# An LSTM grid and a landmark attention in one kernel: LSTM weights, states and row buffers ahead of the group statistics, SP in written order, four edge products at once

## The chip, the cores and the metric

One core of a Trainium2 chip. The metric is the device time of one execution in microseconds (us), lower is better; the time of a kernel is the median of its runs. Profiles show one profiled execution.

## The reference

The input x is 16 images of 64 x 64 pixels with 128 features, in fp32. The reference does three things in a row; each adds its result to its input:

```python
x = x + lstm(group_norm(x))           # two-dimensional LSTM: each pixel needs the pixel above and the one to the left
t = tokens(x)                         # 16 x 4096 x 128
t = t + attention(layer_norm(t))      # 8 heads of 16, 64 landmarks
t = t + ffn(layer_norm(t))            # Wx, batch norm, then y[t] = sigmoid(wx[t] + y[t-1] @ V.T)
```

`group_norm` takes mean and variance for each image over groups of four features and all pixels. The LSTM has five gates, each with weights w (input), u (state) and a bias b. The attention is the Nyström kind: `out = softmax(q kl) @ pinv(softmax(ql kl)) @ (softmax(ql k) @ v)` where ql and kl are means over 64 tokens, and then `res`, a convolution of v along the tokens with 33 taps for each head, is added before the output product.

## The kernel before

All of it runs as one program. TensorE (PE) is the busiest engine; VectorE (DVE), ScalarE (ACT), GpSimd (POOL) and the queue of SyncE (SP) work beside it. The stages follow one another:

1. **Front end.** `attention_tiles` and `conv_bands` (L592) prepare constants of the attention. `conv_bands` writes the taps of each head into a padded line in DRAM (`cb_flat`) and reads it back with overlapping rows into `cb_tm` (L611, on ACT's queue, 128 partitions x 8 heads of 768 bytes). For each head, PE turns it (`cb_t`, L619 to L622) into a band matrix (128 x 128) and two corners, and DVE copies these to `bands` and `edges` (L623, L625). A band product handles what one tile of 128 tokens takes from itself, the corners what it takes from its two neighbours.
2. **Group statistics** (`group_stats`, L32). For each of 16 images a load of 2 MB (`gs_xb`, L56, three buffers) on SP's queue, 32 transposes on PE into banks of PSUM (L61), eight `bn_stats` on DVE (L62), one aggregate (L63). At the end a few small operations, and on POOL the power that gives `grstd` (L29, a helper).
3. **LSTM** (`lstm_grid`, L81). The grid is walked by diagonals; a diagonal of more than 32 pixels is split in two units by images, 190 units in all. A unit has up to four tiles of 128 rows. `load` (L170) fetches x rows (`ls_xt`), `enter` (L175) transposes and normalises them, `gate_x` and `gate_h` (L192, L196) make the gates' products in PSUM, ACT applies sigmoid and tanh (L200), DVE and POOL update cell and state, `turn`, `measure`, `factors` and `normalise` make the output row and its layer norm, `store` (L242) writes it, and `collect` adds it to the landmark sums `acc`. In `slot(t)` (L269) pieces of seven units are interleaved by hand: it loads unit t+5, computes unit t and stores unit t-3. The block `tc.manual_schedule` (L304) keeps PE, DVE, ACT and POOL in the written order. SP is not in the list, so the scheduler places SP's transfers: in the built program the first 18 loads of `ls_xt` stand ahead of the loads of the group statistics, and the LSTM's weights (L105 to L115) and zeroed states (L117 to L123) are issued after the statistics.
4. **Landmarks**: means, inverses.
5. **Attention** (`attention`, L696). An image is eight groups of 512 tokens. `step(s)` (L1061) is written by hand and interleaves several groups: `new` is projected to K, Q and V (`project`, L801) and its largest scores are found (`greatest`, L838), `mid`, one image behind, makes its weights against the landmarks and sums V (`weigh` L865, `values` L884), `nxt` and `cur`, two images behind, compare, soften and attend (L949, L980, L992), `prev` goes on to the next layer (`turn_output`, `feed` L1046). PE, DVE, ACT and POOL keep the written order. PSUM has eight banks of 128 x 512 fp32, each a buffer of its own (`bank(k, ...)`): a product into a bank waits until the last reader of the bank's former content is done.
   In this stage, `project` puts V of a group into bank 2; ACT copies it to SBUF (`at_v`, L814) and DVE copies it in head order to `VH` (`at_vh`, L816), the source of the convolution. `greatest` then uses banks 0, 1, 2, 3. The convolution of a quarter of the heads over half an image is done in each step: `convolve` (L908) makes two band products into one bank (bank 7, or bank 3 in step 3, where it stands in `project`'s `last()` slot), `convolve_edges` (L919) adds four corner products (32 x 32, over two row groups) into the same bank, and ACT copies the bank to `R` (L931). `gather` (L933, bank 4, at the end of an image) and `output` (L1017, bank 6) use other banks.
6. **Recurrence** of the last layer.

The corner products of the kernel before:

```python
first, last = slice(0, E), slice(P - E, P)
for rows, tok, d in ((last, first, -1), (first, last, 1)):
```

Both heads of a pair use the same two row groups of 32 rows, the first and the last.

Of the kernel before, what the change touches and what calls it, by code (L numbers as in the profile page):

```python
# [77 lines left out]
        inv_std(nc, cp, grstd, var, mhalf, "gs")  # L78


def lstm_grid(nc, tc, x, w, u, bias, ident, mhalf, gmean, grstd, t1, acc):  # L81

# [12 lines left out]
    xv = x.rearrange("b i j f -> (i j) b f")  # L95
    tv = t1.rearrange("b n f -> n b f")
    with ExitStack() as ctx:
        cp = ctx.enter_context(tc.tile_pool(name="ls_c", bufs=1))
        ld = ctx.enter_context(tc.tile_pool(name="ls_ld", bufs=AHEAD + 4))
        wk = ctx.enter_context(tc.tile_pool(name="ls_wk", bufs=2))  # L100
        sm = ctx.enter_context(tc.tile_pool(name="ls_sm", bufs=4))
        ps_z = ctx.enter_context(tc.tile_pool(name="ls_psz", bufs=5, space=PSUM))
        ps_t = ctx.enter_context(tc.tile_pool(name="ls_pst", bufs=1, space=PSUM))

        wt, ut, bt = [], [], []  # L105
        for g in range(5):
            a = cp.tile([P, P], F32, name=f"ls_w{g}")
            nc.sync.dma_start(out=a, in_=w[g])
            wt.append(a)
            a = cp.tile([P, P], F32, name=f"ls_u{g}")  # L110
            nc.sync.dma_start(out=a, in_=u[g])
            ut.append(a)
            a = cp.tile([P, 1], F32, name=f"ls_b{g}")
            nc.sync.dma_start(out=a, in_=bias[g].rearrange("(p o) -> p o", o=1))
            bt.append(a)  # L115

        hs = [cp.tile([P, S, D0 + 1, HB], F32, name=f"ls_h{k}") for k in range(2)]  # L117
        cs = [cp.tile([P, S, D0 + 1, HB], F32, name=f"ls_cell{k}") for k in range(2)]
        for a in (*hs, *cs, acc):
            nc.vector.memset(a, 0.0)  # L120
        rows = [cp.tile([P, KT, 2 * F + 4], F32, name=f"ls_tt{k}") for k in range(7)]
        for a in rows:
            nc.vector.memset(a[:, :, F : F + 4], 1.0)  # L123

        class Unit:
            pass
# [175 lines left out]
                    gate_x(after, g)  # L302

        with tc.manual_schedule(  # L304
            engines={mybir.EngineType.PE, mybir.EngineType.DVE, mybir.EngineType.Activation, mybir.EngineType.Pool}
        ):
            for t in range(AHEAD):
                load(units[t])
            for t in range(2):
                enter(units[t])  # L310
            for r in ready[-1]:
                add_states(r)
            for g in (0, 1, 2, 4, 3):
                gate_x(units[0], g)
            for t in range(len(units) + 4):
                slot(t)
# [275 lines left out]
def conv_bands(nc, tc, conv_w, dram, bands, edges):  # L592

    H, _, KS, _ = conv_w.shape
    E = edges.shape[2]
    first = P - 1 + KS // 2
    width = P + 2 * E
    row = P + width  # L600
    with ExitStack() as ctx:
        sp = ctx.enter_context(tc.tile_pool(name="cb_s", bufs=1))
        ps = ctx.enter_context(tc.tile_pool(name="cb_ps", bufs=2, space=PSUM))
        flat = dram.tile([H, row], F32, name="cb_flat")
        line = sp.tile([H, row], F32, name="cb_line")
# [5 lines left out]
        nc.scalar.dma_start(out=tm, in_=bass.AP(tensor=flat.tensor, offset=flat.offset, ap=[[1, P], [row, H], [1, width]]))  # L611
        turn = sp.tile([P, P], F32, name="cb_turn")
        nc.gpsimd.memset(turn, 0.0)
        nc.gpsimd.affine_select(
            out=turn, in_=turn, compare_op=ALU.not_equal, fill=1.0, base=1 - P, pattern=[[1, P]], channel_multiplier=1
        )
        for h in range(H):
            t = ps.tile([P, 2, P], F32, tag="t", name="cb_t")
            nc.tensor.matmul(t[:, 0, :], tm[:, h, E : E + P], turn, start=True, stop=True)  # L619
            before, after = slice(P - E, P), slice(0, E)  # L620
            nc.tensor.matmul(t[before, 1, 0:E], tm[:, h, 0:E], turn[:, 0:E], start=True, stop=True)
            nc.tensor.matmul(t[after, 1, 0:E], tm[:, h, P + E :], turn[:, P - E :], start=True, stop=True)  # L622
            nc.vector.tensor_copy(bands[:, h], t[:, 0, :])  # L623
            for rows in (before, after):
                nc.vector.tensor_copy(edges[rows, h], t[rows, 1, 0:E])  # L625
# [70 lines left out]
def attention(nc, tc, t1, gamma, beta, wqkv, ident, mhalf, fixed, xp, rows, qm, km, pinvT, t2, wx, wx_stats, out):  # L696
# [20 lines left out]
    with ExitStack() as ctx:  # L717
# [10 lines left out]

        bands, edges, wo, bo, wfT, ones, ones_b, minus, ident_b, heads, vs, R, split, tops, avs = fixed

        def quarter(n):
            return slice(n * W2, (n + 1) * W2)

# [67 lines left out]
        def project(gr, last):  # L801

            k, q, v = banks(0, 1, 2)
            nc.tensor.matmul(k, wqkv[:, P : 2 * P], gr.xT, start=True, stop=True)
            gr.KT = big.tile([P, GC], F32, tag="KT", name="at_KT", bufs=Q + 1)
            nc.scalar.copy(gr.KT, k)
            nc.tensor.matmul(q, wqkv[:, 0:P], gr.xT, start=True, stop=True)
            gr.QT = big.tile([P, GC], F32, tag="QT", name="at_QT", bufs=2 * Q + 1)
            nc.scalar.mul(gr.QT, q, 0.25)
            for c in range(C):  # L810
                cs = slice(c * P, (c + 1) * P)
                nc.tensor.matmul(v[:, cs], gr.xT[:, cs], wqkv[:, 2 * P : 3 * P], start=True, stop=True)
            gr.V = big.tile([P, C, F], F32, tag="V", name="at_v", bufs=Q + 1)
            nc.scalar.copy(gr.V.rearrange("p c f -> p (c f)"), v)  # L814
            last()
            nc.vector.tensor_copy(  # L816
                gr.im.VH[:, :, gr.tiles, :].rearrange("p h k d -> p k h d"), v.rearrange("p (k h d) -> p k h d", k=C, h=H)
            )

        def extras(mid, cur):  # L820

# [62 lines left out]
        def values(gr):  # L884


            im = gr.im
            p = bank(6, [P, P])
            for c in range(C):
                for n in range(NP):  # L890
                    nc.tensor.matmul(
                        p[quarter(n)], gr.V[:, c, quarter(n)], gr.e[:, n, c, :],
                        start=(c == 0), stop=(c == C - 1), skip_group_check=True,
                    )
            if gr.g == 0:
                nc.vector.tensor_copy(im.sums, p)
            else:
# [10 lines left out]
        def convolve(im, half, pair, k):  # L908

            lo, hi = half * K // 2, (half + 1) * K // 2  # L910
            im.cv = bank(k, [P, 2, K // 2, DH])
            for j in range(2):
                h = 2 * pair + j

                nc.tensor.matmul(
                    im.cv[:, j], bands[:, h, :], im.VH[:, h, lo:hi], start=(j == 0), stop=True, skip_group_check=True
                )

        def convolve_edges(im, half, pair):  # L919

            lo, hi = half * K // 2, (half + 1) * K // 2
            for j in range(2):
                h = 2 * pair + j
                first, last = slice(0, E), slice(P - E, P)
                for rows, tok, d in ((last, first, -1), (first, last, 1)):
                    a, z = max(lo, -d), min(hi, K - d)
                    nc.tensor.matmul(
                        im.cv[tok, j, a - lo : z - lo], edges[rows, h, :], im.VH[rows, h, a + d : z + d],
                        start=False, stop=True, skip_group_check=True,
                    )  # L930
            nc.scalar.copy(R[:, lo:hi, 2 * pair : 2 * pair + 2, :].rearrange("p k h d -> p h k d"), im.cv)  # L931

        def gather(im):  # L933

            at = bank(4, [P, C, P])
            nc.tensor.transpose(at[:, 0, :], im.sums, ident)
            for n in range(NP):
                nc.tensor.matmul(at[:, 1, W2 * n : W2 * n + 2], im.total[:, n, :], ones[:, 0:2], start=True, stop=True)
# [122 lines left out]
        def step(s):  # L1061
# [309 lines left out]
def kernel(ctx: ExitStack, tc: tile.TileContext, ins: dict, out: bass.AP):  # L1371
# [25 lines left out]
    with tc.tile_pool(name="at_c", bufs=1) as ac, tc.tile_pool(name="at_x", bufs=1) as xp, tc.tile_pool(  # L1397
# [45 lines left out]
```

## Time and profile before

| | |
|---|---|
| median of 3 runs | 4115.65 us (4110.36 to 4120.33) |
| the profiled execution | 4127.1 us, its span 4125.6 us |
| mean granted clock of PE | 0.975 |
| busy in the span | PE 3937.3 (95%), DVE 2956.8 (72%), POOL 2783.7 (67%), ACT 2527.9 (61%) |
| DMA | 383.82 MB in 493553 packets, mean 93 GB/s |

The stages in the trace, by windows (us from the start): 0 to 113 front end and group statistics, 113 to 1520 LSTM, 1520 to 1718 landmarks, 1718 to 1840 the first 16 steps of the attention, 1840 to 3600 its steady part, 3600 to 3815 its end, 3815 to 4126 the recurrence.

How to read rows of the profile: a row of a timeline has the start in us, the length in us of what is grouped, the engine, the line of the program, the operation, output and input, the shapes and the count; in brackets stands how long the engine was idle before, and which instruction it waited for. SPq and ACTq are the queues on which SP and ACT issue transfers; PEld is the loading of weights into PE, which overlaps PE's products. The ends of products overlap, so the cost of a piece of PE's work is read from its start to the next piece's start.

### The profile page before, as it was taken

To read this page: it belongs to the slowest core of one execution; us is meant where nothing else is said; L and a number is where in the kernel's file an instruction comes from. 1 tells how busy PE (TensorE), PEld (TensorE's weight loads), DVE (VectorE), ACT (ScalarE), POOL (GpSimd) and SP (SyncE) were. 2 spreads that over 40 slices of the span, in tenths; PEclk is the share of its full clock that TensorE was granted. 3 is DMA by queue.
4 is the path that set the end of the run, shared out by engine and by line. 5 is a ranking of instruction groups with operands and counts; after the bars stand their busy time and mean duration, and the time that the engine had idled before them with its cause. 6 is when DMAs were issued, how large, how long until landed. Compare 5 with 4: busy or idle time off the path is not lost. (4 is left out here: it accounts for less than half of the span.)

```text
span 4125.6 us, 99034 instructions
## 1 busy us (share of the span) xinstructions
PE 3937.3 (95%) x37518; PEld 2651.4 (64%) x37518; DVE 2956.8 (72%) x7152; ACT 2527.9 (61%) x4973; POOL 2783.7 (67%) x4189
## 2 busy tenths in 40 slices
PE   7899999999999989889999999999999999988697
PEld 5767665555667678656666666666666666655486
DVE  8677777777787775437777777777777777757465
ACT  0466655555666654346666666666666666755597
POOL 0577776777777763247878778787877788787133
PEclk9799999999999989999999999999999999999798
DMA  8123222223232210112333332333333233222799
GB/s 341 43 69 81 78 76 78 78 79 83 76 82 77 72 40 4 45 32 77 83 90 86 86 92 80 92 82 90 88 84 93 80 93 82 81 73 82 234 265 174
DMA packets 493553, 383.82 MB, mean 93 GB/s; under 512 B 35208, under 2 KB 466192, under 8 KB 491024
## 3 DMA queue, kind: packets, MB, share of 16 engines
q1 hardware_dynamic: 473840, 341.82, 28.7%
q0 software_dynamic: 17728, 34.61, 4.7%
q8 instruction: 299, 4.90, 0.5%
q14 instruction: 182, 1.49, 0.1%
q10 hardware_dynamic: 1504, 0.99, 0.1%
HBM read 172.82 MB, written 204.48 MB: 91 GB/s over the span
## 5 line engine op out<-in xcount | busy, mean ns | idle before, releaser
L200 ACT ACTIVATE ls_g<-ls_z,ls_b 128x304 f32<-128x304 f32 (+26 forms) x950 | 509.1, 548 | 372.5 <-PE ls_z L198 336.0
L906 POOL TENSOR_TENSOR at_total<-at_total,at_e 128x512 f32<-128x512 f32 x480 | 611.0, 1273 | 131.7 <-ACT at_e L882 102.8
L194 PE MATMUL ls_z<-ls_xn,ls_w 128*128 128x304 f32 (+26 forms) x1900 | 611.3, 470 | 8.2 <-DMA ls_w<-in_L_conv_wf_dram 5.2
L194 PEld LDWEIGHTS ls_z<-ls_xn,ls_w 128*128 128x128 f32 x1900 | 341.8, 196 | 184.5 <-issue 84.6
L778 POOL TENSOR_SCALAR at_T<-at_T,at_nb 128x128 f32<-128x128 f32 x512 | 403.5, 796 | 13.3
L845 DVE TENSOR_REDUCE at_mxq<-at_bank 128x1 f32<-128x512 f32 x512 | 328.6, 683 | 113.0 <-PE at_bank L842 112.9
L198 PE MATMUL ls_z<-ls_hsum,ls_u 128*128 128x304 f32 (+26 forms) x1140 | 371.6, 463 | 0.0
L280 POOL TENSOR_TENSOR ls_g<-ls_g,ls_cell 128x304 f32<-128x304 f32 (+26 forms) x190 | 175.8, 926 | 280.9 <-ACT ls_g L200 256.0
L961 DVE TENSOR_REDUCE at_cmx<-at_bank 128x8 f32<-128x512 f32 x512 | 317.6, 684 | 59.0 <-PE at_bank L954 58.6
L882 ACT ACTIVATE at_e<-at_bank 128x512 f32<-128x512 f32 x512 | 264.3, 603 | 114.1 <-PE at_bank L876 114.1
L990 ACT ACTIVATE at_eT<-at_bank 128x512 f32<-128x512 f32 x512 | 264.3, 603 | 95.7 <-PE at_bank L987 95.7
L198 PEld LDWEIGHTS ls_z<-ls_hsum,ls_u 128*128 128x128 f32 x1140 | 213.8, 196 | 128.6 <-issue 78.2
L237 ACT ACTIVATE ls_tt<-ls_tt,ls_nb 128x128 f32<-128x128 f32 (+9 forms) x632 | 261.0, 479 | 4.1 <-POOL ls_nb L232 4.1
L198 PE MATMUL ls_z<-ls_h,ls_u 128*128 128x304 f32 (+26 forms) x760 | 259.9, 465 | 2.1 <-DVE ls_h L288 1.9
L228 POOL TENSOR_TENSOR ls_tt<-ls_ve,mhalf 128x4 f32<-128x4 f32 (+2 forms) x190 | 228.5, 1203 | 15.2
L281 DVE TENSOR_TENSOR ls_g<-ls_g,ls_g 128x304 f32<-128x304 f32 (+26 forms) x190 | 98.4, 518 | 194.7 <-POOL ls_g L280 193.5
L1259 DVE SCALAR_TENSOR_TENSOR rc_y<-rc_w,rc_scale,rc_z 128x256 f32<-128x256 f32 x344 | 155.3, 481 | 108.1 <-PE rc_z L1246 107.1
L1246 PE MATMUL rc_z<-rc_y,rc_vT 128*128 128x256 f32 x688 | 186.0, 408 | 40.4 <-ACT rc_y L1267 28.8
L816 DVE COPY at_vh<-at_bank 128x512 f32<-128x512 f32 x128 | 88.5, 692 | 185.9 <-ACT at_v L814 154.6
L1042 ACT ACTIVATE at_z<-at_u,at_nb,at_r 128x128 f32<-128x128 f32 x512 | 211.6, 504 | 11.5 <-POOL at_nb L1037 11.5
L229 POOL TENSOR_TENSOR ls_tt<-ls_ve,mhalf 128x4 f32<-128x4 f32 (+2 forms) x190 | 214.3, 1128 | 0.0
L1052 ACT COPY at_fx<-at_bank 128x512 f32<-128x512 f32 x128 | 132.7, 1037 | 125.5 <-DVE wx_stats L1050 100.4
(249 smaller groups left out, 9651.3 us busy)
## 6 DMA issues: line engine op xcount, KB each, us to landing
t<-ls_tt SPq DMA_DIRECT2D x392, 130.0 KB
at_T<-t SPq DMA_DIRECT2D x128, 264.0 KB
gs_xb<-in_x_dram SPq DMA_DIRECT2D x16, 2048.0 KB
at_xh<-t SPq DMA_DIRECT2D x128, 256.0 KB
t<-at_u SPq DMA_DIRECT2D x128, 256.0 KB
out_dram<-at_u SPq DMA_DIRECT2D x128, 256.0 KB
wx<-at_fx SPq DMA_DIRECT2D x128, 256.0 KB
rc_w<-wx SPq DMA_DIRECT2D x64, 512.0 KB
```

Of the source, the lines that this page charges most:

```text
L194: nc.tensor.matmul(v.z[g][:, : v.cols], wt[g], v.xn, start=True, stop=False)
L198: nc.tensor.matmul(view(v, v.z[g]), ut[g], hin, start=False, stop=True)
L200: nc.scalar.activation(a[:, : v.cols], v.z[g][:, : v.cols], AF.Tanh if g == 4 else AF.Sigmoid, bias=bt[g])
L228: nc.gpsimd.tensor_tensor(v.tt[:, 0:k, F + 2], ve[:, 0, :k], mhalf[:, :k], ALU.pow)
L229: nc.gpsimd.tensor_tensor(v.tt[:, 0:k, F + 3], ve[:, 1, :k], mhalf[:, :k], ALU.pow)
L237: nc.scalar.activation(v.tt[:q, k, F + 4 :], v.tt[:q, k, 0:F], AF.Identity, bias=v.nb[:q, k : k + 1], scale=v.tt[:q, k, F + 3 : F + 4],)
L778: nc.gpsimd.tensor_scalar(x[:, c, :], x[:, c, :], gr.nbt[:, 0, c : c + 1], gr.nbt[:, 1, c : c + 1], ALU.mult, ALU.subtract)
L845: nc.vector.tensor_reduce(gr.im.mxq[:, n : n + 1, gr.g], gr.s[n], AX.X, ALU.max)
L882: nc.scalar.activation(gr.e[:, n].rearrange("p c m -> p (c m)"), s[n], AF.Exp)
L906: nc.gpsimd.tensor_tensor(total, total, e[:, :, c, :], ALU.add)
L961: nc.vector.tensor_reduce(gr.mx[:, n].rearrange("p j c -> p c j"), gr.s[n].rearrange("p (c j m) -> p c j m", c=C, j=2), AX.X, ALU.max)
L990: nc.scalar.activation(gr.eT[:, n], s[n], AF.Exp)
```

## The change

- **LSTM.** Weights, biases, zeroed states and row buffers become a function of their own, `lstm_tiles`. It is called before `group_stats`, in a pool that is opened before it; the weights are now issued on ACT's queue. The zeroing of `acc` stays in `lstm_grid`.
- **SP in written order**: `group_stats` runs in a block that keeps SP in order, and the LSTM's block has SP in its list. The LSTM's pools get their waits by tile. In the built program, the statistics' loads `gs_xb` now stand ahead of the x rows of the LSTM; the first three do not wait for PE, and the first load of x rows waits for the last readers of the statistics' memory.
- **VH** is copied from `gr.V` in SBUF instead of from the bank, in three copies; odd heads get the two halves of the partitions exchanged, and `conv_bands` makes their bands and corners to match (two half-height products in place of one for an odd head).
- **Convolution**: the two heads of a pair go to two banks (7 and half of the bank 6 that `values` uses; 2 and 3 in step 3), and the four corner products use four different row groups. `R` is filled by two ACT copies, one for each bank. `values` leaves its sums in bank 6 until after the convolution (`keep_values`). `output` moves from bank 6 to 4, `gather` from 4 to 5.

```diff
+def lstm_tiles(nc, cp, shape, w, u, bias):
...
+        nc.scalar.dma_start(out=a, in_=w[g])
...
+    for a in (*hs, *cs):
+        nc.vector.memset(a, 0.0)
...
-def lstm_grid(nc, tc, x, w, u, bias, ident, mhalf, gmean, grstd, t1, acc):
+def lstm_grid(nc, tc, x, fixed, ident, mhalf, gmean, grstd, t1, acc):
...
-        ld = ctx.enter_context(tc.tile_pool(name="ls_ld", bufs=AHEAD + 4))
+        ld = ctx.enter_context(tc.tile_pool(name="ls_ld", bufs=AHEAD + 4, reuse_waits="tile"))
...
         with tc.manual_schedule(
-            engines={mybir.EngineType.PE, mybir.EngineType.DVE, mybir.EngineType.Activation, mybir.EngineType.Pool}
+            engines={
+                mybir.EngineType.PE, mybir.EngineType.DVE, mybir.EngineType.Activation, mybir.EngineType.Pool,
+                mybir.EngineType.SP,
+            }
         ):
+            nc.vector.memset(acc, 0.0)
...
-            before, after = slice(P - E, P), slice(0, E)
+            before, after = ((slice(mid - E, mid), slice(mid, mid + E)) if mid else (slice(P - E, P), slice(0, E)))
...
-            nc.vector.tensor_copy(
-                gr.im.VH[:, :, gr.tiles, :].rearrange("p h k d -> p k h d"), v.rearrange("p (k h d) -> p k h d", k=C, h=H)
-            )
+            to = gr.im.VH[:, :, gr.tiles, :].rearrange("p (n j) k d -> p j k n d", j=2)
+            by = gr.V.rearrange("p k (n j d) -> p j k n d", j=2, d=DH)
+            nc.vector.tensor_copy(to[:, 0], by[:, 0])
+            for rows, other in ((low, high), (high, low)):
+                nc.vector.tensor_copy(to[rows, 1], by[other, 1])
...
-            p = bank(6, [P, P])
+            gr.six = bank(6, [P, 2, 2 * P])
+            p = gr.six[:, 0, 0:P]
...
-            im.cv = bank(k, [P, 2, K // 2, DH])
+            im.cv = [a.rearrange("p (k d) -> p k d", d=DH) for a in of]
...
-                first, last = slice(0, E), slice(P - E, P)
-                for rows, tok, d in ((last, first, -1), (first, last, 1)):
+                for rows, tok, d in ((quarter(3 - 2 * j), quarter(0), -1), (quarter(2 * j), quarter(3), 1)):
...
-            nc.scalar.copy(R[:, lo:hi, 2 * pair : 2 * pair + 2, :].rearrange("p k h d -> p h k d"), im.cv)
+            for j in range(2):
+                nc.scalar.copy(R[:, lo:hi, 2 * pair + j, :], im.cv[j])
...
-            at = bank(4, [P, C, P])
+            at = bank(5, [P, C, P])
...
-            p = bank(6, [P, C, F])
+            p = bank(4, [P, C, F])
...
-                    convolve(*conv, 3)
+                    convolve(*conv, [a[:, 0 : 2 * P] for a in banks(2, 3)])
...
-                convolve(*conv, 7)
+                convolve(*conv, [bank(7, [P, 2 * P]), mid.six[:, 1] if mid else bank(6, [P, 2 * P])])
+            if mid:
+                keep_values(mid)
...
-            group_stats(nc, tc, x, ident, mhalf, gmean, grstd)
...
-            lstm_grid(nc, tc, x, *lw, ident, mhalf, gmean, grstd, t1, acc)
+            with tc.tile_pool(name="ls_c", bufs=1) as lc:
+                lstm_fixed = lstm_tiles(nc, lc, (B, D0, F), *lw)
+                with tc.manual_schedule(engines={mybir.EngineType.SP}):
+                    group_stats(nc, tc, x, ident, mhalf, gmean, grstd)
+                lstm_grid(nc, tc, x, lstm_fixed, ident, mhalf, gmean, grstd, t1, acc)
```

More of the change, by code (lines that the diff above doesn't have):

```diff
@@ L78, in group_stats @@
         inv_std(nc, cp, grstd, var, mhalf, "gs")
-def lstm_grid(nc, tc, x, w, u, bias, ident, mhalf, gmean, grstd, t1, acc):
+def lstm_tiles(nc, cp, shape, w, u, bias):
+    B, D0, F = shape
+    S = 2
+    HB = B // S
+    KT = D0 * HB // P
+    wt, ut, bt = [], [], []
+    for g in range(5):
+        a = cp.tile([P, P], F32, name=f"ls_w{g}")
+        nc.scalar.dma_start(out=a, in_=w[g])
+        wt.append(a)
+        a = cp.tile([P, P], F32, name=f"ls_u{g}")
+        nc.scalar.dma_start(out=a, in_=u[g])
+        ut.append(a)
+        a = cp.tile([P, 1], F32, name=f"ls_b{g}")
+        nc.scalar.dma_start(out=a, in_=bias[g].rearrange("(p o) -> p o", o=1))
+        bt.append(a)
+    hs = [cp.tile([P, S, D0 + 1, HB], F32, name=f"ls_h{k}") for k in range(2)]
+    cs = [cp.tile([P, S, D0 + 1, HB], F32, name=f"ls_cell{k}") for k in range(2)]
+    for a in (*hs, *cs):
+        nc.vector.memset(a, 0.0)
+    rows = [cp.tile([P, KT, 2 * F + 4], F32, name=f"ls_tt{k}") for k in range(7)]
+    for a in rows:
+        nc.vector.memset(a[:, :, F : F + 4], 1.0)
+    return wt, ut, bt, hs, cs, rows
+def lstm_grid(nc, tc, x, fixed, ident, mhalf, gmean, grstd, t1, acc):
     B, D0, D1, F = x.shape
@@ L97, in lstm_grid @@
     with ExitStack() as ctx:
-        cp = ctx.enter_context(tc.tile_pool(name="ls_c", bufs=1))
-        ld = ctx.enter_context(tc.tile_pool(name="ls_ld", bufs=AHEAD + 4))
[L100 to L123, printed above, removed]
+        ld = ctx.enter_context(tc.tile_pool(name="ls_ld", bufs=AHEAD + 4, reuse_waits="tile"))
+        wk = ctx.enter_context(tc.tile_pool(name="ls_wk", bufs=2, reuse_waits="tile"))
+        sm = ctx.enter_context(tc.tile_pool(name="ls_sm", bufs=4, reuse_waits="tile"))
+        ps_z = ctx.enter_context(tc.tile_pool(name="ls_psz", bufs=5, space=PSUM, reuse_waits="tile"))
+        ps_t = ctx.enter_context(tc.tile_pool(name="ls_pst", bufs=1, space=PSUM, reuse_waits="tile"))
+        wt, ut, bt, hs, cs, rows = fixed
         class Unit:
@@ L618, in conv_bands @@
             t = ps.tile([P, 2, P], F32, tag="t", name="cb_t")
-            nc.tensor.matmul(t[:, 0, :], tm[:, h, E : E + P], turn, start=True, stop=True)
-            before, after = slice(P - E, P), slice(0, E)
+            mid = P // 2 if h % 2 else 0
+            for i in range(0, P, mid or P):
+                n, c = mid or P, E + (i + mid) % P
+                nc.tensor.matmul(t[i : i + n, 0, :], tm[:, h, c : c + n], turn, start=True, stop=True)
+            before, after = ((slice(mid - E, mid), slice(mid, mid + E)) if mid else (slice(P - E, P), slice(0, E)))
             nc.tensor.matmul(t[before, 1, 0:E], tm[:, h, 0:E], turn[:, 0:E], start=True, stop=True)
@@ L729, in attention @@
         bands, edges, wo, bo, wfT, ones, ones_b, minus, ident_b, heads, vs, R, split, tops, avs = fixed
+        low, high = slice(0, P // 2), slice(P // 2, P)
         def quarter(n):
@@ L884, in values @@
         def values(gr):
-            im = gr.im
-            p = bank(6, [P, P])
+            gr.six = bank(6, [P, 2, 2 * P])
+            p = gr.six[:, 0, 0:P]
             for c in range(C):
@@ L894, in values, with keep_values @@
                     )
+        def keep_values(gr):
+            im, p = gr.im, gr.six[:, 0, 0:P]
             if gr.g == 0:
@@ L906, in add_weights, with convolve @@
                 nc.gpsimd.tensor_tensor(total, total, e[:, :, c, :], ALU.add)
-        def convolve(im, half, pair, k):
+        def convolve(im, half, pair, of):
             lo, hi = half * K // 2, (half + 1) * K // 2
-            im.cv = bank(k, [P, 2, K // 2, DH])
+            im.cv = [a.rearrange("p (k d) -> p k d", d=DH) for a in of]
             for j in range(2):
@@ L915, in convolve @@
                 nc.tensor.matmul(
-                    im.cv[:, j], bands[:, h, :], im.VH[:, h, lo:hi], start=(j == 0), stop=True, skip_group_check=True
+                    im.cv[j], bands[:, h, :], im.VH[:, h, lo:hi], start=True, stop=True, skip_group_check=True
                 )
@@ L923, in convolve_edges @@
                 h = 2 * pair + j
-                first, last = slice(0, E), slice(P - E, P)
-                for rows, tok, d in ((last, first, -1), (first, last, 1)):
+                for rows, tok, d in ((quarter(3 - 2 * j), quarter(0), -1), (quarter(2 * j), quarter(3), 1)):
                     a, z = max(lo, -d), min(hi, K - d)
                     nc.tensor.matmul(
-                        im.cv[tok, j, a - lo : z - lo], edges[rows, h, :], im.VH[rows, h, a + d : z + d],
+                        im.cv[j][tok, a - lo : z - lo], edges[rows, h, :], im.VH[rows, h, a + d : z + d],
                         start=False, stop=True, skip_group_check=True,
                     )
-            nc.scalar.copy(R[:, lo:hi, 2 * pair : 2 * pair + 2, :].rearrange("p k h d -> p h k d"), im.cv)
+            for j in range(2):
+                nc.scalar.copy(R[:, lo:hi, 2 * pair + j, :], im.cv[j])
         def gather(im):
-            at = bank(4, [P, C, P])
+            at = bank(5, [P, C, P])
             nc.tensor.transpose(at[:, 0, :], im.sums, ident)
```

## The prediction

> **What bounds the kernel now.** I cut the span into stages first (busy time by window; columns: window, length, then busy time of PE, PEld, DVE, ACT, POOL, granted clock, DMA share, GB/s).
>
> ```profile
> 0.00:113.00 113.00, 86.07 (x565) 62.82 (x565) 91.67 (x190) 0.00 (x0) 2.71 (x15) 1.00 0.78 312
> 1840.00:3600.00 1760.00, 1749.62 (x21163) 1157.44 (x21165) 1331.29 (x2849) 1204.18 (x2240) 1395.97 (x2207) 1.00 0.31 85
> ```
>
> In steady attention (14 of the 16 images, 125.56 us each) PE is busy 1749.62 of 1760 us: a step costs what PE's pieces cost, from start to start, and these include waits too short to show as idle. So I read PE's timeline over one step (15.47 us).
>
> ```profile
> 2508.18 1.48 PE L842 MATMUL at_bank<-at_KT,qm 32*128 32x512 f32 x8
> 2509.58 1.07 PE L997 MATMUL at_bank<-at_eT,at_heads 128*32 128x512 f32 x8
> ...
> 2516.66 1.05 PE L927 MATMUL at_bank<-at_vh,edges 32*32 32x256 f32 x8
> 2517.64 0.40 PE L985 MATMUL at_bank<-at_topT,at_minus 32*128 32x512 bf16 x4
> 2517.87 1.03 PE L987 MATMUL at_bank<-at_QT,km 32*128 32x512 f32 x8
> 2518.72 1.06 PE L954 MATMUL at_bank<-km,at_QT 32*128 32x128 f32 x32
> ```
>
> The greatest-product (L842) takes 1.40, the same shape at L987 .85; the edges (L927) take .98. Why L842 is long, from the timeline of DVE and of the weight loads:
>
> ```profile
> 2507.78 0.69 DVE L816 COPY at_vh<-at_bank 128x512 f32<-128x512 f32 x1 [0.95 <-ACT at_v L814]
> ...
> 2508.52 0.30 PEld L842 LDWEIGHTS at_bank<-at_KT,qm 32*128 32x128 f32 x4 [0.16 <-DVE at_vh L816]
> ```
>
> The third product needs bank 2, which the DVE copy L816 still reads, and that copy starts only after ACT's copy of the same bank. In steps 0 and 3 of an image, where nothing is late, L842 takes .97.
>
> The front end, from the timelines of the queues and of PE and DVE:
>
> ```profile
> 4.32 13.58 SPq L173 DMA_DIRECT2D ls_xt<-in_x_dram x18
> 6.03 0.40 ACTq L611 DMA_DIRECT2D cb_tm<-cb_flat x1
> ...
> 10.76 0.77 PE L619 MATMUL cb_t<-cb_turn,cb_tm 128*128 128x128 f32 x2 [10.76 <-DMA cb_tm<-cb_flat]
> ...
> 27.66 0.70 DVE L62 BATCH_NORM_STATS2 gs_st<-gs_tp 128x6 f32<-128x512 f32 x1 [7.06 <-PE gs_tp L61]
> ```
>
> The statistics' 2 MB loads are issued at 18.72; from 27.66 to 110.78 DVE sets 5.14 us an image (8 x .60 + .37). Then the start of the LSTM:
>
> ```profile
> 116.83 0.33 SPq L108 DMA_DIRECT2D ls_w<-in_L_conv_wf_dram x1
> ...
> 125.90 1.28 ACT L200 ACT_TABLE_LOAD   x1 [125.90 <-PE ls_z L198]
> 127.19 0.93 ACT L200 ACTIVATE ls_g<-ls_z,ls_b 128x16 f32<-128x16 f32 x5
> ```
>
> **Attention: VH copied from SBUF.** Bank 2 is then free when ACT's L814 ends, 2507.75, before PE gets to L842. The stall goes: 1.40 to .97, −.44 x 6 steps = −2.64 an image. In its place come three DVE copies of 256 elements. The nearest rows are PSUM copies, .29 at 128 and .692 at 512 columns, so .43 each, 1.27 for three; .28 each if SBUF is read faster, .85. In steady steps DVE waits .76 for L842 right after, so +.16 to +.58 is covered. Without that cover, in the ramp's first eight steps, the chain L814, VH, L845, L788, L794, L804 sets the period (7.06 us): 8 x (.15 to .6) = +1.2 to +4.7, and I take +3.
>
> **Attention: four edge products at once.** Eight instructions (four products, two fp32 passes) of 256 columns take .98 today. A full-height product of 256 columns takes .243 a pass (L915: .97 for four), so one by one they would take 1.94: they run two by two. L987 shows four row groups at once (eight instructions of 512 columns in .85). Four together: 2 x .243 and some .06 of fill = .55, so −.43. Here the Trainium skill ("TensorEngine Tiling (Array Packing)", Gotcha 1: PSUM Pressure) speaks against it: different row tiles cannot use one PSUM bank at the same time. After the change two row groups still share each of the two banks. By the rule, there is no gain beyond what two banks give, and the edges stay at .98. But at L927 all four row groups share one bank and pairs overlap all the same. I take the row.
>
> Given back: the copy of the result into R becomes two ACT copies of 256 (.373 each, between .266 at 128 and .586 at 512 columns) behind L1052. With T the start of L1049 (2514.82), L1052 ends at T+2.87 and the second copy at T+3.67; bank 6 holds its source, and L954's third product, now due at T+3.48, needs bank 6: about +.17 (0 to .25) in steps 0, 1, 2, 4, 5, 6. So the edges bring −.26 x 6 = −1.56. Step 7: the gather goes to bank 5 and waits for L1052 (T+2.94) where PE would come .55 earlier: +.12 net. Step 3: the early convolution uses banks 2 and 3 and waits for L814, +.76 against −.43: +.33. An image: −2.64 −1.56 +.12 +.33 = −3.75, range −2.3 (edges not overlapped) to −4.7 (nothing given back). Times 14: −52.5. The other eight ramp steps gain nothing (L804 waits for ACT's xT there), the last steps about −1. Attention: −52.5 +3 −1 = **−50.5** (−32 to −66). The other engines allow it: POOL works 12.2 of the new 14.7-us step, DVE 11.7, ACT 10.6.
>
> **Start of the LSTM.** Weights, zeroed states and row buffers are ready long before, so PE's waits for ls_w (.67, .77, 2.25) and four .93 memsets leave this stretch. Against that, the pool of x rows now lies on the statistics' memory and the first row load waits for their last readers, grstd's POOL power among them: it is issued at 116.85, the very place ls_w had. Rows land 2.05 later (ls_w, 116.83 to 118.88), then transposes, DVE .17, POOL .22, ten gate products (2.4): first gate at about 123.45 where it was 127.19. The table load no longer waits behind PE. **−3.7** (−1 to −5). SP's written order from there: in the middle of the LSTM a slot lasts 9.85, SP issues four stores (2.8) and four loads (2.1), and the loads run three slots ahead. Behind a waiting store stand only loads not needed for three slots: 0. The waits of the row loads for DVE (449.5 us of them on SP's queue, all covered) vanish, worth 0.
>
> **Front end.** The LSTM weights follow cb_tm on ACT's queue and wait for PE's last reading of cb_tm; nothing there is due for 90 us: 0. But the statistics' loads no longer wait for PE. The first three (6 MB) go at 4.3, 4.8 and 6.0, so they are in the engines when cb_tm (768-byte rows, 64 for each engine) is issued at 6.03. Until cb_tm lands, PE cannot start the bands, DVE's order holds bands and edges ahead of the statistics, and all 16 images stand behind. The LSTM's memsets and wfT (4.9 us) now follow the edges too, and acc's .91 falls among the statistics; PE has four banks filled by then (−1.2). If cb_tm keeps 10.76: first statistics at 19.4 + 4.9 = 24.3, the end 3.6 earlier. If bytes are shared evenly: cb_tm about 2 later, −1.6. The trace of before has no two queues full at once at this place; with one queue alone cb_tm took 4.7 from issue to PE. The rule that bears on it is the Trainium skill's ("DMA: Bandwidth & Descriptors", Queues, rings and completion order): an engine alternates between queues packet by packet and drains a whole packet before it switches. The statistics' packets are 16 KB (the page counts 2529 packets of 8 KB or more; 2048 are these loads), eight an engine and load; at the measured 440 GB/s over 16 engines, .6 us each. About 21 are left against cb_tm's 64, so cb_tm would land only after all three loads, near 23.5: +12.8 on the bands, first statistics at 37.1 and their end 83.5 − .3 later, 120.3 instead of 111.15: **+9.2**. I take the rule, since cb_tm's small rows are what loses in any sharing by turns; −3.6 is the other bound.
>
> **Sum.** −50.5 −3.7 +9.2 = −45.0. The profiled execution took 4127.1 (span 4125.6), so 4082.1 there; it lies 11.4 above the median 4115.65, so **4071** in medians.
>
> **Rivals.**
> - *cb_tm is hardly delayed* (−3.6 to −1.6 instead of +9.2): 4115.65 −50.5 −3.7 −2.5 = 4059. For it: cb_tm is only .8 MB. Against: the whole packets. Chance .30.
> - *The edges gain nothing*, because the tiling rule holds or because the two R copies hold bank 6 for the .43 won: six steps lose 1.56, attention −50.5 + 14 x 1.56 = −28.7, in all −23.2, 4092. For it: the bank rule. Against: L927's own pairs. Chance .12.
> - *Slower: SP in written order starves the LSTM.* Its issues take 4.9 of 9.85 us a slot. It decides only if SP's issues with their waits exceed the slot: at twice the rows' cost, 9.8, nothing is lost yet; at 2.3 times, 11.3, each of some 60 full slots loses 1.4, +84 and 4155. Against it: the same instructions are issued today at the rows' cost. Chance .03.
> - *The VH copies are not covered*: 1.27 ends later than PE's need. That returns at most .4 x 6 x 14 = 34: 4105. Against: L845 is the next DVE work and waits for PE. Chance .05.
>
> **How the numbers follow.** Likeliest, .50: 4071, its own range 4056 to 4087. Adding the first two rivals gives 4043 to 4096 as the range, which leaves out the last two and the far tails of attention's −32 and −66. This kernel's runs lie within .25%, so about .2% (8 us) is what can be told from no change: faster .95, same .02, slower .03.
>
> **What would show it.** L842's group at .97 from start to start in all steps; L927's at .55; a step of 14.6 to 14.75 and an image of 121.8; a short wait of L954 for ACT's R copy. In the front end the first cb_t product near 23 and first statistics near 37 (11 and 24 by the rival); first row load right after grstd; table load before the first gate; first gate 12.7 us after the last aggregate instead of 16.4. I am wrong if L842 still waits, if edges stay at .98, or if LSTM slots show PE waiting for ls_xt.

## The result, and the profile after

The changed kernel takes 4086.02 us (median of 4 runs, 4077.8 to 4091.27) against 4117.99 before (4 runs): ratio .9923, interval .9900 to .9946. It is faster by 32 us where 45 were forecast. The profiled execution took 4091.3, 35.8 less than the one before, and I account for these 35.8 below.

PE's timeline of one steady attention step after the change, the pieces that answer to those shown of before (L951 are the corners, L864 the greatest-product):

```profile
2580.52 0.63 PE L951 MATMUL at_bank<-at_vh,edges 32*32 32x240 f32 x8
2581.09 0.40 PE L1010 MATMUL at_bank<-at_topT,at_minus 32*128 32x512 bf16 x4
...
2587.10 1.03 PE L864 MATMUL at_bank<-at_KT,qm 32*128 32x512 f32 x8
2588.06 1.07 PE L1022 MATMUL at_bank<-at_eT,at_heads 128*32 128x512 f32 x8
```

From start to start the corners take .57 (forecast .55, before .98) and L864 .96 (forecast .97, before 1.40). A steady step takes 14.62, an image 121.2 (forecast 121.8, before 125.55).

The front end, from the timelines of SP's and ACT's queues, PE and DVE:

```profile
3.89 3.27 SPq L56 DMA_DIRECT2D gs_xb<-in_x_dram  x3
...
7.04 0.40 ACTq L625 DMA_DIRECT2D cb_tm<-cb_flat  x1
...
24.07 0.77 PE L637 MATMUL cb_t<-cb_turn,cb_tm 128*128 128x128 f32 x2 [24.07 <-DMA cb_tm<-cb_flat]
...
37.18 0.68 DVE L62 BATCH_NORM_STATS2 gs_st<-gs_tp 128x6 f32<-128x512 f32 x1
```

cb_tm waits behind the statistics' loads as forecast (23.5 and 37.1 in the prediction). The view of the DMA queues from 13 to 16 us shows how (packets, MB, share of the 16 engines; q1 is SP's queue, q10 ACT's):

```profile
q1 hardware_dynamic: 76, 1.25, 96.7%
q10 hardware_dynamic: 75, 0.06, 5.6%
```

76 packets of 16 KB and 75 of 768 bytes: one for one. The turns by packets are seen at work, and cb_tm's packets pay .6 us of another queue for each of their own (96.7% of 16 engines for 3 us, shared by 76 packets).

What was not forecast stands at the start of the attention. PE's timeline of one of its first eight steps, before the change and then after it:

```profile
1747.16 1.12 PE L804 MATMUL at_bank<-at_xT,wqkv 128*128 128x512 f32 x2 [0.93 <-ACT at_xT L794]
...
1749.96 1.13 PE L842 MATMUL at_bank<-at_KT,qm 32*128 32x512 f32 x4
1751.43 1.13 PE L842 MATMUL at_bank<-at_KT,qm 32*128 32x512 f32 x4 [0.34 <-DVE at_vh L816]
1752.63 0.66 PE L788 MATMUL at_bank<-ident,at_xh 128*128 128x128 f32 x4
```

```profile
1739.81 2.08 PE L824 MATMUL at_bank<-at_xT,wqkv 128*128 128x512 f32 x2 [0.93 <-ACT at_xT L814]
1741.68 1.92 PE L827 MATMUL at_bank<-at_xT,wqkv 128*128 128x512 f32 x2
...
1744.99 1.87 PE L864 MATMUL at_bank<-at_KT,qm 32*128 32x512 f32 x8
1747.98 1.07 PE L808 MATMUL at_bank<-ident,at_xh 128*128 128x128 f32 x4 [1.12 <-DVE at_mxq L867]
```

The same K product (two instructions of 512 columns) takes 1.12 before and 2.08 after: PE runs at half clock. The step takes 10.17, from one K product to the next, in place of 7.06. (Before, one of the eight steps takes 8.74, with a K product of 1.68: PE fell to half clock there too, once.) The windows of these steps give the granted clock (the number after POOL's busy time), first before, then after:

```profile
1731.00:1780.00 49.00, 39.86 (x186) 20.01 (x190) 19.96 (x33) 17.50 (x29) 1.44 (x7) 0.97 0.15 38
```

```profile
1731.00:1795.00 64.00, 51.69 (x151) 26.93 (x151) 20.11 (x42) 16.38 (x26) 0.00 (x0) 0.66 0.10 26
```

By the stage, against before: last aggregate +8.5; first gate of the LSTM −3.2 from there; LSTM +3.0 (+3.4 in its first twelve units); landmarks −3.7 (the same code; in their second 40 us the granted clock is .96 where it was .91); first nine attention steps +23.4; to the end of the ramp, the first 16 steps, −2.3; thirteen steady images −56.1; tail and recurrence −5.4. Sum −35.8.

### The profile page after: what moved, and what is told of

Same layout as the page of the kernel before. It is cut to its first block, busy times and chain, and to the rows that moved or that the text cites. A ratio compares the mean times of both kernels' runs of the same rounds, so it can differ in the third digit from the quotient of the medians.

```text
span 4089.7 us, 99565 instructions
## 1 busy us (share of the span) xinstructions
PE 3870.2 (95%) x37526; PEld 2621.9 (64%) x37526; DVE 2983.5 (73%) x7408; ACT 2519.4 (62%) x5101; POOL 2809.3 (69%) x4189
## 5 line engine op out<-in xcount | busy, mean ns | idle before, releaser
L1267 POOL DMA_DIRECT2D out_dram<-rc_tt x64 | 77.4, 1209 | 189.5 <-ACT rc_tt L1264 186.7
```

## The experiments

Theory: the first attention steps run at half clock because the copy of VH from SBUF puts a long wait in place of a short one (before, L842 waits .34 for DVE; after, L808 waits 1.12 for DVE; next to each stands .93 for ACT), and this, not the copies' own length, eats the gain; cb_tm's delay is the front end's cost. Rival: the half clock comes from the phase of the stages ahead, that is, from when and how they end. Each run is compared with runs of before on the same chip, so ratios are read, not microseconds across tables. All but front_only start from the changed kernel. A first step is read from K product to K product, the clock over a window inside these steps.

| run | what differs | ratio to before | first steps | granted clock there |
|---|---|---|---|---|
| changed kernel | | .9923 (.9900 to .9946) | 10.17 | .66 |
| front_only | attention of before | 1.0017 (1.0008 to 1.0027) | 7.06 | .97 |
| att_only | front end and LSTM of before | .9892 (.9877 to .9908) | 10.17 | .68 |
| ramp_psum | VH of image 0 from bank 2 | .9906 (.9889 to .9922) | 7.78 and 9.30 in turn | .89 |
| ramp_fill | 512 columns of idle work | .9866 (.9850 to .9883) | 7.38 | 1.00 |
| fill_128 | 128 columns of idle work | one run, 4077.6 us | 7.39, two of 9.06 | .95 |
| ramp_bank | next rows' transposes in bank 5 | .9860 (.9843 to .9876) | 6.19 | 1.00 |
| cbtm_first | cb_tm ahead of the loads | .9883 (.9864 to .9902) | 10.16 | .66 |
| edges_pairs | corners on two row groups | .9993 (.9982 to 1.0003) | 7.28 to 9.9 | .78 |
| xrows | first x rows early | .9903 (.9884 to .9923) | 8.8 to 10.2 | .69 |
| warm_start | products before the LSTM | one run, 4089.6 us | 7.9 to 10.2 | .73 |
| best | three repairs | .9846 (.9832 to .9859) | 6.19 | 1.00 |
| best2 | the same, x rows spread | .9829 (.9816 to .9843) | 6.19 | 1.00 |

### The parts by themselves: front_only, att_only

> The changed front end and LSTM with the attention of before. Theory (the half clock in the first attention steps comes with the new VH copy): these steps keep 7.06 us as before; last aggregate at about 119.3 as after the change; in all some 8 us over before, about 4126. Rival (the half clock comes from the phase of the stages ahead of the attention, not from its code): the first eight steps take about 10.2 us here too, about 4146.

> The changed attention (and bands) with the front end and LSTM of before. If the parts of the change don't touch each other, this is the changed kernel less the 8 us of the front end: some 40 below before, ratio .990. If the half clock of the first attention steps depends on what runs ahead of them, the first steps differ from 10.17 here: at 7.3 the ratio would be .985.

The edits exchange `conv_bands` and `attention`, or all else, for those of before. front_only came out as expected: +.17%, about 7 us, last aggregate at 119.2, and the first attention steps keep 7.06. att_only has 10.17 with the front end of before. So the half clock comes with the changed attention, not with the phase: the rival falls. The product of both ratios, .9909, agrees with the changed kernel's .9923 within its interval: nothing shows that the parts touch each other.

### The half clock: ramp_fill, fill_128, ramp_psum, ramp_bank

ramp_fill and fill_128 (there with 128 columns of bank and KT) add one product that nobody reads:

```diff
+                if s < Q:
+                    nc.tensor.matmul(bank(7, [P, GC]), ident, new.KT, start=True, stop=True)
```

> The changed kernel with one product of 512 columns more in each of the first eight attention steps, into a bank that nobody reads, right where PE waits 1.12 us for DVE. It adds work only. Theory (PE's long idle lets the clock fall): the clock stays above .9, steps near 7.3, about 20 below the changed kernel, 4066. Rival (phase, or PE's idle is not the cause): half clock as before it, steps 10.2 or more, 4086 or a few more.

> The same filling as with 512 columns, but a product of 128 columns: .13 us of work in the 1.12 us. If any product in the stretch is enough, steps are near 7.3 at full clock. If it is the share of work that counts, they stay near 10.2 at half clock, because .13 changes the share little. I expect the second.

ramp_psum:

```diff
-            by = gr.V.rearrange("p k (n j d) -> p j k n d", j=2, d=DH)
+            src = v.rearrange("p (c f) -> p c f", c=C) if gr.im.b == 0 else gr.V
+            by = src.rearrange("p k (n j d) -> p j k n d", j=2, d=DH)
```

> The changed kernel, but image 0 copies VH from bank 2 as before (in three copies); all other images from SBUF. Theory: the first eight attention steps go back to 7.1 to 7.4 us at a granted clock above .9, in all 20 to 24 below the changed kernel, about 4064; the ninth step on as after the change, 14.62 a steady step. Rival (phase): they stay near 10.2, about 4086.

ramp_bank:

```diff
-                turn_rows(after)
+                turn_rows(after, 5 if s < Q - 1 else 1)
```

> The changed kernel, but in the first seven attention steps the transposes of the next rows go to bank 5 in place of bank 1, so that PE does not wait for DVE's reductions there. Theory (PE's idle stretch of 1.12 us lowers the clock): only the .93 wait for ACT's xT is left, full clock, a step is PE's pieces, .96 + .86 + .98 + .97 + .44 + .93 = about 5.2 instead of 10.17; in all about 34 below the changed kernel, ratio to before .984. Rival (half clock stays whatever PE waits for): pieces twice as long, about 8.5 to 9 a step, 8 to 12 below the changed kernel.

PE's timeline of one of the first steps of ramp_fill (L1131 is the added product), and then the clock in the window of the changed kernel's steps above in fill_128, ramp_psum and edges_pairs (of which more below), in this order:

```profile
1762.41 1.87 PE L864 MATMUL at_bank<-at_KT,qm 32*128 32x512 f32 x8
1764.22 1.12 PE L1131 MATMUL at_bank<-at_KT,ident 128*128 128x512 f32 x2
1765.41 0.66 PE L808 MATMUL at_bank<-ident,at_xh 128*128 128x128 f32 x4
1766.99 0.70 PE L824 MATMUL at_bank<-at_xT,wqkv 128*128 128x512 f32 x1 [0.93 <-ACT at_xT L814]
```

```profile
1731.00:1795.00 64.00, 50.05 (x266) 27.34 (x268) 27.17 (x58) 22.59 (x37) 1.89 (x8) 0.95 0.18 45
1731.00:1795.00 64.00, 49.00 (x181) 23.84 (x182) 26.78 (x50) 19.61 (x32) 1.46 (x7) 0.89 0.14 35
1731.00:1795.00 64.00, 50.09 (x178) 26.84 (x177) 23.03 (x50) 18.76 (x30) 1.46 (x7) 0.78 0.12 29
```

Work that nobody needs, put where PE waits, makes the kernel 23 us faster than the changed one (.9866 against .9923). So the wait causes the half clock. fill_128 did not come as I expected: .13 us of products are enough for most steps (in one run). ramp_psum came halfway: three copies from PSUM take 1.28 where one took .69, so PE waits 1.04 before its third product, and every second step falls to half clock.

Sorted by the waits of PE that the timeline shows, as a share of a step at full clock, the granted clock falls in one order (one trace of each):

| | shown waits | of a step of | share | granted clock |
|---|---|---|---|---|
| ramp_fill | .93 | 7.38 | 13% | 1.00 |
| ramp_bank | .93 | 6.19 | 15% | 1.00 |
| before | .34 + .93 | 7.06 | 18% | .97 |
| fill_128 | .71 + .93 | 7.38 | 22% | .95 |
| ramp_psum | 1.04 + .93 | 7.78 | 25% | .89 |
| edges_pairs | 1.02 + .93 | 7.28 | 27% | .78 |
| changed kernel | 1.12 + .93 | 7.38 | 28% | .66 |

The stage stood near an edge, and the change pushed it over. The longest wait by itself does not give this order: ramp_psum waits longer at a stretch than edges_pairs and has the higher clock. What the clock answers to is not shown. The shown waits are not all of PE's waiting: at full clock the changed step is only .3 longer than before, so about .5 of the .8 by which they grew lay before inside L842, where the modelled ends of its products hide it. And another stretch grew with them: from the end of the greatest-product to the next K product, in which PE does nothing but four transposes. By the modelled ends it is 1.66 in the step of before (1752.56 to 1754.22) and 3.12 in the changed one (1746.86 to 1749.98). No run separates the two.

The copies' own cost shows where the changed code runs at full clock, as once in warm_start (below), from transposes to transposes; L811 there is L808:

```profile
1778.36 0.66 PE L811 MATMUL at_bank<-ident,at_xh 128*128 128x128 f32 x4 [1.12 <-DVE at_mxq L870]
...
1785.75 1.12 PE L811 MATMUL at_bank<-ident,at_xh 128*128 128x128 f32 x4 [1.13 <-DVE at_mxq L870]
```

That is 7.39, and 7.38 in ramp_fill: .32 a step more than the 7.06 of before. edges_pairs, whose copies do not exchange the halves, runs such steps in 7.28.

ramp_bank removes the wait instead of filling it:

```profile
1762.32 1.87 PE L864 MATMUL at_bank<-at_KT,qm 32*128 32x512 f32 x8
1764.12 0.66 PE L808 MATMUL at_bank<-ident,at_xh 128*128 128x128 f32 x4
1765.70 1.13 PE L824 MATMUL at_bank<-at_xT,wqkv 128*128 128x512 f32 x2 [0.93 <-ACT at_xT L814]
```

It keeps the full clock, but at 6.19, not 5.2: my 5.2 took L864 at .97, while here its third product waits for ACT's copy out of bank 2, and L864 takes 1.80. In the steady step `weigh` lies between the two and hides that wait. In the eighth step, where the edit leaves the transposes in bank 1, PE waits 1.13 again, and the ninth takes 12.32 in place of 9.71.

### The front end: cbtm_first, xrows, warm_start

cbtm_first issues the three transfers up to cb_tm on SP's queue and puts them and the statistics in one ordered block:

```diff
-        nc.scalar.dma_start(out=flat, in_=line)
+        nc.sync.dma_start(out=flat, in_=line)
...
+        in_order = tc.manual_schedule(engines={mybir.EngineType.SP})
+        in_order.__enter__()
```

> The changed kernel with the three small transfers up to cb_tm on SP's queue, in order ahead of the statistics' loads. Theory (cb_tm stands behind three loads of 2 MB by turns of packets): first cb_t product at about 11 instead of 24.1, first statistics at 24.3 instead of 37.2, 12.9 less: 4073. Rival (the statistics' loads that now go last become what is waited for): the first of them lands near 16 to 18, which is before 24, so at most some us are lost again; if first statistics come at 30 or later, the rival holds, 4079 or more.

First cb_t product at 13.53 instead of 24.07, first statistics at 26.63 instead of 37.18, last aggregate 9.75 earlier, and .9883 in all. The 2.5 us short of my 11 are the chain on SP: cb_flat is issued at 6.11, on ACT's queue at 3.80. The first statistics come 13.1 after the first cb_t product in both, so the loads, now last, cost nothing there.

xrows moves the pool of x rows out of the statistics' memory and loads five units after the third load of the statistics:

```diff
+            if b == 3:
+                rows_of_lstm()
...
-        sp = ctx.enter_context(tc.tile_pool(name="gs_s", bufs=2))
+        sp = ctx.enter_context(tc.tile_pool(name="gs_s", bufs=1))
```

> The changed kernel with the pool of x rows outside the statistics' memory and the loads of the first five units issued behind the third of the statistics' loads. Theory: no landing of 2.05 us between grstd and the first products; the first gate is 9.5 to 10.5 us after the last aggregate instead of 13.2, so 3 less in this place; in all 3 less, give or take the 3 to 5 of the clock's phase at the start of the LSTM. Rival (the landing is covered by other work): first gate as before it at 13.

The first gate comes 9.6 after the last aggregate (13.2 changed): −3.6, as expected. The whole shows none of it, because of the second edit (there was no space for two buffers of `st`): each image then takes 5.39 instead of 5.14, and the last aggregate is 4.8 later.

warm_start:

```diff
+            for t in range(4):
+                z = ps_z.tile([P, NC], F32, tag="z", name="ls_z")
+                nc.tensor.matmul(z, ident, ident[:, None, :].to_broadcast([P, KT, P]), start=True, stop=True)
```

> The changed kernel with four products of 512 columns (into a bank that nobody reads) while PE waits for grstd and the first x rows. If the half clock at the start of the LSTM is only the result of PE's idle time before it, the first eight units run at full clock, 3 to 3.5 us each instead of 5.2 to 5.7, and the twelfth unit is 12 to 16 us earlier. If the small products of these units (16 to 112 columns) can't hold the full clock by themselves, the units fall back to 5.2 and the twelfth unit stands within 3 us of where it stands in the changed kernel (192.7). I expect the second, because PE shows no idle time in these units and still stays at half clock.

PE's timeline of it:

```profile
121.83 6.17 PE L324 MATMUL ls_z<-ident 128*128 128x512 f32 x8
...
129.41 1.55 PE L203 MATMUL ls_z<-ls_xn,ls_w 128*128 128x16 f32 x10
130.79 1.01 PE L207 MATMUL ls_z<-ls_h,ls_u 128*128 128x16 f32 x4
...
133.35 2.34 PE L203 MATMUL ls_z<-ls_xn,ls_w 128*128 128x32 f32 x10
```

Ten products take 1.55 in the first unit (2.32 in the changed kernel) and 2.34 in the second: the full clock lasts for one unit. The window of the first units in the changed kernel shows PE busy all the time at a clock of .50:

```profile
132.00:171.00 39.00, 39.00 (x182) 36.04 (x182) 17.71 (x83) 16.85 (x53) 16.71 (x45) 0.50 0.07 20
```

Unit 12 (its tanh of the cell) stands at 189.7 against 192.7 in the changed kernel, but at 190.3 in front_only and ramp_psum, which have the same code there without the four products: little or nothing of this is their gain. Where the first units return to full clock by themselves differs from run to run (158 us before, 171 in the changed profile). From the first gate to unit 12 it is 60.3 in the changed profile, 58.2 to 58.3 in front_only, ramp_psum, cbtm_first and warm_start, and 56.8 and 56.9 in before and att_only. So of the +3.4 some 2.0 is the clock of one execution, and 1.4 comes with the changed front end.

### The corners: edges_pairs

```diff
-                for rows, tok, d in ((quarter(3 - 2 * j), quarter(0), -1), (quarter(2 * j), quarter(3), 1)):
+                for rows, tok, d in ((quarter(3), quarter(0), -1), (quarter(0), quarter(3), 1)):
```

> The changed kernel, but both heads of a pair use the first and last row groups for the corners again (halves not exchanged in VH, bands whole); banks, copies of R and all else as changed. Theory: the corners take .98 instead of .57, a steady step 15.03 instead of 14.62 (less where the copy of R was waited for), an image 2.4 to 3 more, in all 34 to 42 over the changed kernel, ratio to before about 1.001. Rival (the corners' gain is not from the row groups but from the two banks): step stays at 14.62.

PE's timeline:

```profile
2584.93 1.05 PE L951 MATMUL at_bank<-at_vh,edges 32*32 32x240 f32 x8
2585.92 0.39 PE L1010 MATMUL at_bank<-at_topT,at_minus 32*128 32x512 bf16 x4
```

.99 for the corners with the two banks as changed: the gain is from the four row groups. A step takes 15.02, an image 124.04. So VH from SBUF, with all that the two banks cost, is worth 1.5 an image, and the row groups 2.8. Without the row groups nothing of the whole change can be told from no change (.9993).

### The repairs together: best, best2

> Three repairs of the changed kernel together: cb_tm in order ahead of the statistics' loads on SP's queue, the first x rows loaded during the statistics (pool of eight buffers in place of nine, outside the statistics' memory), and the transposes of the first attention steps in bank 5. If their gains add up (10.5 at the front end, 3.6 at the LSTM's start, 24 to 29 in the first attention steps), some 38 to 43 below the changed kernel: ratio to before .982 to .983. If the clock's phase at the start of the LSTM or in the landmarks takes part of it, .984 to .987.

> The three repairs as before, with one difference: the first x rows are issued one unit after each of the statistics' loads 4 to 8, not ten transfers in a row ahead of the fourth load. In the earlier version the fourth load came only at 41.7 us and PE waited 10.3 us for it. Theory (a step put into an ordered queue costs what stands behind it): the last aggregate is back at 109.5 as with cb_tm first alone, 8.5 earlier than in the earlier version; ratio to before .9820 to .9830. Rival (the x rows disturb the loads wherever they stand): last aggregate at 114 or later, ratio .984 or more.

best put ten loads of x rows ahead of the fourth load of the statistics on the ordered queue: that load was issued at 41.74, PE waited 10.3 for it, and the last aggregate came at 118.0. best2 issues one unit after each of the loads 4 to 8:

```diff
+            if 4 <= b < 9:
+                rows_of_lstm(b - 4)
```

Its last aggregate is at 110.78 (1.3 later than cbtm_first's, as PE still waits for some of the loads), the first gate 9.6 later, a first step 6.19; .9829, 4054.74 us, .9% faster than the changed kernel and 1.7% than before.

## Why the prediction was right in kind and 15 us off

- **VH from SBUF, steady: right.** L864 at .96, no wait for DVE; −.44 a step as forecast.
- **Corners: right in mechanism, and cheaper than forecast.** −.41 for a forecast −.43. The rule that row tiles can't share a bank (the Trainium skill, "TensorEngine Tiling (Array Packing)", Gotcha 1) was rightly set aside: the four run together with two in each bank. One reading was wrong: at L927 it is two row groups, not four, that share the one bank. **The term given back was mis-sized**: L979 does wait for the second copy of R (10.4 us in 65 waits of the weight loads), but these loads run ahead of the products, and the step shows none of the +.17: it loses .85, all of .44 + .41. Step 3 costs +.52 and not +.33 (16.05 for 15.53); step 7 +.21 and not +.12. An image: −2.64 −2.46 +.52 +.21 = −4.37, measured −4.35, instead of −3.75: 14 x .6 = 8 us better than forecast.
- **The VH copies "without that cover, in the ramp's first eight steps … I take +3": the step that failed.** The copies cost .32 a step (7.38 against 7.06), inside the stated .15 to .6, and 8 x .32 = 2.6 is near the +3. But the sum held each of PE's pieces at its duration of before. At half clock the first nine steps cost +23.4. I had the granted clock in the windows (.97 in these steps, .99 over the ramp) and did not ask what a longer wait does to it. This one term is 20 us.
- **Front end: right.** +8.5 for a forecast +9.2; cb_tm's packets alternate one for one with the statistics' packets (75 against 76 in 3 us), as the Trainium skill says ("DMA: Bandwidth & Descriptors", Queues, rings and completion order). The rival "hardly delayed" falls.
- **Start of the LSTM: right at the first gate, −3.2 for −3.7, but less of it lasts.** The first row load goes out at 125.76, right behind grstd (122.78 and 2.96 long), and the table load is at 106.55, off the path. But the second unit's gates follow the first's by 3.4 before and by 4.7 after, so from the last aggregate to them the gain is 1.9. (Before, the five gates of the first unit follow the late table load at once, .93 in all; after, they follow PE's products, from 132.49 to 134.20.) SP's written order costs nothing: from unit 12 to the end the LSTM's distance to before goes from 8.7 to 8.3.
- **The rivals**: the edges did gain; the slower case (SP starving the LSTM) did not come; the VH copies are covered in the steady steps.
- **Sum**: 20 worse in the first nine attention steps; 10 better in the rest of the attention and after it, 8 of them in the steady images; the other stages 1 better in all, though the LSTM's +3.0 and the landmarks' −3.7 stood in no term: −45 became −36 in the profile and −32 in the medians. That the miss is 15 and not 25 is luck: a gain put too low made up for part of a cost that was not seen.

## What to carry to other kernels

When an edit removes a short wait of PE and leaves a longer one in the same stage, price the stage at the half clock too, above all where PE has little work: here .8 us more of shown waiting in a step cost 3.1, of which the copies are .3 and the clock is 2.8, and a product of .13 us that nobody reads gave most of it back. A large load that no longer waits for its turn takes the turns of the small ones: issue the small transfer that others wait for first, as cbtm_first does on the same queue. In a queue kept in order, spread a group of small transfers among the large ones: in a row ahead of one load they cost 7.2 us here (last aggregate at 118.0 against 110.78).

## What the runs showed of the hardware

- A PE that is busy 80% of the time by the profile (51.69 of 64 us) can stand at a granted clock of .66; with 1.27 us of waits in a step of 7.06 it had .97. The Trainium skill ("TensorE: Matmul & The Clock Gate", A second HAM failure mode: psum-queue depth-cycling) tells of a kernel whose clock goes up and down because PE idles briefly between groups of products; the page's table of goals (Why this matters for your kernels) warns only of gaps above some 3 us. No wait that the timeline shows in these steps is longer than 1.13, and the clock fell all the same; if four transposes count as part of a gap, it is 3.12, and no run shows whether they do.
- In the LSTM's first units PE shows no idle time between products of 16 to 112 columns and stays at half clock all the same (39.00 of 39 us busy, .50); four products of 512 columns before them gave the full clock for one unit. That column count is what the clock answers to is argued, not shown.
- Corner products of two row groups in each of two PSUM banks ran four at once (.57 for eight instructions, .99 on two row groups). Two row groups in one bank overlap as well (L927 before: .98 for eight, where one by one would take 1.94 by the prediction's estimate). In both, the two row groups of a bank write different partitions of it; no run has them write the same.
